# Output stores begun by ScalarE's queue instead of SyncE's, in a two-layer graph kernel

## The chip, the cores and the metric

The kernel runs on one core of a Trainium2 chip. Time is the device time of one execution in microseconds (us), smaller is better; a value is the median of several runs. The engines are TensorE (PE in the profile, with its weight loads as PEld), VectorE (DVE), ScalarE (ACT), GpSimd (POOL) and SyncE (SP). A "q" behind an engine's name means its instruction sequencer: DMA issues appear as SPq or ACTq.

## What is computed

x has 32 batches of 512 rows by 1024 columns, adj is 512 by 512, all in float32. The reference, cut to what matters:

```python
def layer0(h, wq, wk, adj, bm):            # h: (32, 512, 1024)
    q = einsum('c,bcn->bn', wq, h); k = einsum('c,bcn->bn', wk, h)
    s = leaky_relu(q[:, None, :] + k[:, :, None], 0.01)
    agg = einsum('bcn,bmn->bcm', h, softmax(s, -1))
    return relu(einsum('oc,bcm->bom', adj, agg) + bm[None, :, None])

x = x + layer0(relu(layernorm(x)), wq, wk, adj, bm)
h = relu(layernorm(x))
x = x + einsum('bnf,nm->bmf', h, adj * adj) + bias
return x
```

In layer 1 the weight W is adj squared element by element.

## The kernel before

A batch is four row tiles of 128 by 1024. The attention of layer 0 is not formed as a 1024 by 1024 matrix. Since the score is a leaky relu of a sum, the softmax splits into two sums over sorted keys. So a batch goes through these steps (the names are those of the functions and of the profile's tiles):

- `load` (L309, SP): four tiles of x. `stats`, `norm`, `slopes`, `relu` (L334 to L366): layer norm and relu.
- `scores` (L375): q and k by TensorE, copied by ScalarE (qr, L380) and stored by ScalarE's queue to DRAM (qd, L381); `row` (L386) loads them back from ScalarE's queue, broadcast over all partitions (qrow). `rank` (DVE) and `lower` (ScalarE, L433) count, for each column, its place in the sorted order.
- `value` (L474): TensorE multiplies h by adj; `spread` (L481, ScalarE) copies each result out of PSUM; `scatter` (L487, GpSimd) writes the rows in sorted order to a table in DRAM (td).
- `fetch` (L503, SP) reads the sorted table back (vs) in three pieces of 792 KB. `scan` (L559, L562) makes running sums in nine steps. In `sums` (L572 to L581) ScalarE copies a step's result out of PSUM into a tile t of a pool with two buffers. One row of it for each half is carried into the next step's operand, by ScalarE copies (L572, L573) in the first five and last four batches, and by two small SP transfers (L576, L577) in those between; two SP transfers (L580, L581) store t to the table.
- `gather` (L586, GpSimd) reads for each column three table rows (g, a pool with one buffer); `excess`, `divide`, `weigh` (L611, ScalarE), `combine` (L615, DVE) put them together; `turn` (L622, TensorE, then L626, DVE) transposes them and adds them to a second copy of x that `reload` (L314, SP) has brought (y in the profile).
- Layer 1: `stats`, `norm` and `relu` again (L337 to L366); `propagate` and `finish` (L657, L670, L674) multiply by W in a scheme with seven products, and in the last four batches `sow`, `plain` and `close` (L685, L689, L696) in the ordinary way. DVE adds each PSUM result to y in place.
- `store` (L701): when DVE has added the last piece to a row tile of y, that tile of 512 KB is written to the output. Four stores a batch, 128 in all.

The order of the work is written out by hand: ORDER is a long string of two-character codes, each of which names the next step of one lane (a step of the list above with its place in the batch). The steps of five to six batches are interleaved. The scheduler is told to keep this order (`tc.manual_schedule`), so each engine's instructions stand in its program in the order in which the steps call them, and an engine runs its program in order. A DMA is an instruction in the program of the engine that begins it, with its waits. SP begins loads, reloads, fetches, carry rows, table stores and output stores: 1442 DMAs. ScalarE begins 67, among them L381 and L386. Both engines' DMAs take eight completion semaphores in turn, in the order of the steps; a DMA waits until the earlier one with its semaphore has landed, whichever engine began that one. Tiles x, y, h and mx share a pool of 16 row buffers, so a store's landing also frees a buffer for a later load.

In a batch of the long middle part the stores stand as follows. Row 1 stands between the first and second L366 of a batch five ahead, and three loads follow it in SP's program. Row 2 stands before a copy L574, and carry rows follow it. Row 3 stands between L381 and L481. Row 0 stands between the second and third L337 of the following batch.

Of the kernel before, what the change touches and what calls it, by code (L numbers as in the profile page):

```python
# [16 lines left out]
P = 128  # L17
# [143 lines left out]
def kernel(  # L161
# [32 lines left out]
    nc = tc.nc  # L194
# [503 lines left out]
        )  # L698

    def store(s, c):  # L700
        nc.sync.dma_start(out[s.b, ts(c, P), :], s.x[c])  # L701

    lanes = {}

# [7 lines left out]
    for b in range(B):  # L712
        s = Batch()
# [37 lines left out]
        else:  # L751
            for f in (sow, plain, close):
                plan(s, f, f.__name__, args=all_of(NC, range(NH)))
        plan(s, store, "store", count=NC)
        plan(s, combine, "combine", args=all_of(NN, (1, 2)))
    names = list(lanes)
    for code in ORDER.split():
        for k in range(0, len(code), 2):
# [3 lines left out]
            s, t = args[0], len(steps)  # L762
# [31 lines left out]
```

## Time and profile before

| | us |
|---|---|
| median of 3 runs | 2302.11 (2301.16 to 2302.13) |
| profiled execution | 2301.56 |
| its span, first to last instruction | 2299.8 |
| busy: PE / ACT / DVE / POOL | 2215.1 / 1730.8 / 1719.3 / 716.9 |
| DMA | 657.77 MB, mean 286 GB/s |
| granted TensorE clock, mean | 0.988 |

| queue | begun by | share of the 16 DMA engines' time |
|---|---|---|
| q1 | SP | 46.7% |
| q0 | GpSimd (scatter, gather) | 31.3% |
| q10 | ScalarE | 2.8% |

How to read the profile's rows. A row of the timeline has the start in us from the span's beginning, the length in us, the engine, the line of the kernel, the operation, what it writes and reads with the shapes, and how many instructions are merged in it; the bracket is how long the engine stood open before and what ended that. A row of the waits has the waiting engine and line, what released it, the total in us, the number of times and the longest. A row of a stage has its bounds, its length, the busy time of PE, PEld, DVE, ACT and POOL with counts, then the granted clock, the DMA engines' mean busy share and GB/s. A row of a DMA queue has packets, MB, and the share of the 16 engines' time.

### The profile page before, as it was taken

How to read it: one execution, taken by the hardware profiler on the slowest of the kernel's cores; microseconds unless marked ns; L12 is line 12 of the kernel's file. 1: busy time of each engine (PE TensorE's matmuls, PEld its weight loads, DVE VectorE, ACT ScalarE, POOL GpSimd, SP SyncE). 2: the span in 40 equal slices, each digit the busy share in tenths (PEclk: the TensorE clock that was granted, in tenths of full speed). 3: DMA queues.
4: the chain of work that ended last, by engine and by line, in shares of the span. 5: the costliest groups of instructions: out<-in, count | busy, mean ns of one | idle time of the engine just before them, and what ended most of it. 6: DMA issues, size and time to landing. Idle time of an engine off the chain costs nothing.

```text
span 2299.8 us, 28792 instructions
## 1 busy us (share of the span) xinstructions
PE 2215.1 (96%) x7344; PEld 946.6 (41%) x7344; DVE 1719.3 (75%) x4840; ACT 1730.8 (75%) x3317; POOL 716.9 (31%) x979
## 2 busy tenths in 40 slices
PE   6978999999999999999999999999999999999897
PEld 3423443444444444444444444344444444443343
DVE  6746777878778778877877877877877787777453
ACT  4699889776778777777877777877777887787752
POOL 2343223333323333233333222333332333224210
PEclk9989999999999999999999999999999999999999
DMA  6676878888889888888888878888888888877961
GB/s 225 234 282 232 282 293 309 313 298 295 274 291 324 296 311 291 286 291 317 308 310 298 298 267 310 317 301 305 294 275 290 323 300 305 311 246 277 356 243 64
DMA packets 217717, 657.77 MB, mean 286 GB/s; under 512 B 39376, under 2 KB 39504, under 8 KB 217552
## 3 DMA queue, kind: packets, MB, share of 16 engines
q1 hardware_dynamic: 153760, 362.16, 46.7%
q0 software_dynamic: 57344, 276.86, 31.3%
q10 hardware_dynamic: 6448, 16.92, 2.8%
q8 instruction: 59, 0.97, 0.2%
q14 instruction: 106, 0.87, 0.1%
HBM read 438.05 MB, written 217.01 MB: 285 GB/s over the span
## 4 chain that ended last, share of the span: by engine, by line
PE 77%; DMA 8%; ACT 6%; DVE 5%; issue 2%; POOL 1%; SPq 0%; ACTq 0%; POOLq 0%; DVEq 0%
PE pv L474 34%; PE pg L657 26%; PE sc L562 9%; PE tr L622 3%; DMA td<-t 3%; PE pq L375 2%; DVE g L615 2%; DMA g<-td,idg 2%; PE pp L689 1%; PE sc L559 1%; ACT junk L433 1%; DVE y L626 1%; ACT junk L337 1%; DMA td<-v,idx 1%; DMA vs<-t 1%
## 5 line engine op out<-in xcount | busy, mean ns | idle before, releaser
L474 PE MATMUL pv<-wmT,x 128*128 128x512 f32 x2048 | 917.5, 596 | 0.0
L474 PEld LDWEIGHTS pv<-wmT,x 128*128 128x128 f32 x2048 | 380.5, 190 | 489.1 <-issue 452.1
L487 POOL DMA_INDIRECT td<-v,idx x256 | 270.7, 1057 | 659.5 <-issue 283.5
L657 PE MATMUL pg<-h,wsq 128*128 128x512 f32 x896 | 412.4, 602 | 2.5 <-DVE y L674 2.0
L615 DVE SCALAR_TENSOR_TENSOR g<-g,cf 128x512 f32<-128x512 f32 x512 | 375.2, 764 | 17.2 <-ACT g L611 14.0
L586 POOL DMA_INDIRECT g<-td,idg x256 | 244.8, 956 | 299.2 <-DVE y L626 95.2
L433 ACT ACTIVATE junk<-qrow,qk 128x1024 uint8<-128x1024 f32 x256 | 292.8, 1144 | 30.3 <-DMA qrow<-qd 19.9
L562 PE MATMUL sc<-vs,sm 128*64 128x512 f32 x1024 | 284.0, 621 | 7.8 <-ACT vs L572 5.8
L657 PEld LDWEIGHTS pg<-h,wsq 128*128 128x128 f32 x896 | 163.3, 190 | 243.3 <-issue 180.9
L574 ACT COPY t<-sc 128x512 f32<-128x512 f32 x288 | 167.6, 582 | 99.2 <-PE sc L562 41.6
L481 ACT COPY v<-pv 128x512 f32<-128x512 f32 x256 | 147.4, 578 | 124.3 <-PE pv L474 77.4
L546 POOL TENSOR_TENSOR sm<-mask_a,wc 128x192 f32<-128x192 f32 x96 | 63.2, 658 | 521.4 <-PE sc L562 455.9
L657 PE MATMUL pg<-mx,wmix 128*128 128x512 f32 x448 | 209.4, 599 | 0.0
L366 ACT ACTIVATE x<-x,nmr,rstd 128x1024 f32<-128x1024 f32 x128 | 149.3, 1230 | 78.2 <-DVE nmr L359 78.2
L670 DVE SCALAR_TENSOR_TENSOR y<-pg,bm_sb,y 128x512 f32<-128x512 f32 x224 | 166.4, 745 | 45.9 <-PE pg L657 45.5
L422 DVE TENSOR_SCALAR_CACHE_REDUCE junk<-qrow,qk,cnt 128x128 uint8<-128x128 f32 (+6 forms) x224 | 180.4, 805 | 8.2
L626 DVE SCALAR_TENSOR_TENSOR y<-tr,nbm,y 128x512 f32<-128x512 f32 x256 | 174.7, 746 | 15.3 <-PE tr L622 12.4
L417 DVE TENSOR_SCALAR_CACHE_REDUCE junk<-qrow,qk 128x896 uint8<-128x896 f32 (+6 forms) x224 | 165.7, 740 | 18.6 <-DMA qrow<-qd 16.7
L674 DVE TENSOR_TENSOR y<-pg,y 128x512 f32<-128x512 f32 x168 | 115.1, 685 | 81.6 <-PE pg L657 81.1
L611 ACT ACTIVATE g<-g,cf 128x512 f32<-128x512 f32 x256 | 168.6, 709 | 3.4 <-DVE cf L605 1.7
L337 ACT ACTIVATE junk<-y,nm 128x1024 uint8<-128x1024 f32 x128 | 146.7, 1146 | 31.4 <-DVE nm L345 29.6
L366 ACT ACTIVATE h<-y,nmr,rstd 128x1024 f32<-128x1024 f32 x128 | 154.0, 1235 | 2.6 <-DVE nmr L359 2.6
(135 smaller groups left out, 2496.4 us busy)
## 6 DMA issues: line engine op xcount, KB each, us to landing
vs<-td SPq DMA_DIRECT2D x96, 792.0 KB
td<-t SPq DMA_DIRECT2D x576, 132.0 KB
x<-in_x_dram SPq DMA_DIRECT2D x128, 512.0 KB
y<-in_x_dram SPq DMA_DIRECT2D x128, 512.0 KB
out_dram<-y SPq DMA_DIRECT2D x128, 512.0 KB
qrow<-qd ACTq DMA_DIRECT2D x32, 512.0 KB
vs<-t SPq DMA_DIRECT2D x368, 2.0 KB
td<-v,idx POOLq DMA_INDIRECT x256, 6.3
```

The costliest lines, as they stand in the source:

```text
L337: nc.scalar.activation(junk, s.x[c], AF.Square, bias=s.nm[:, c : c + 1], scale=1.0 / ROOT, accum_out=s.var[:, c : c + 1],)
L366: nc.scalar.activation(h, s.x[c], AF.Relu, bias=s.nmr[:, c : c + 1], scale=s.rstd[:, c : c + 1])
L422: nc.vector.tensor_scalar(junk[:, j * P :], s.qrow[:, j * P :], qc, first, ALU.is_lt, ALU.add, accum_out=s.cnt[:, 1, j : j + 1],)
L433: nc.scalar.activation(junk, s.qrow, AF.Sign, bias=s.qk[:, 1, j : j + 1], accum_out=s.sgn[:, j : j + 1])
L474: nc.tensor.matmul(pv, s.h[c][:, ts(j, P)], wmT[:, c, :], start=(c == 0), stop=(c == NC - 1))
L487: i = nc.gpsimd.indirect_dma_start(tds[s.b % TABLES][:, :], bass.IndirectOffsetOnAxis(ap=s.idx[j // 4][:, j % 4 : j % 4 + 1], axis=0), v[: ...
L562: nc.tensor.matmul(p[ts(k, HP), :], m[:, k, :], s.vs[h][:, 0:C], start=True, stop=True)
L586: nc.gpsimd.indirect_dma_start(s.g[:, j, :], None, tds[s.b % TABLES].rearrange("(s k) w -> s k w", k=3), bass.IndirectOffsetOnAxis(ap=s.id ...
L611: nc.scalar.mul(r, r, s.cf[:, 0, j : j + 1])
L615: nc.vector.scalar_tensor_tensor(r, s.g[:, j, k * W : k * W + C], s.cf[:, k, j : j + 1], r, ALU.mult, ALU.add)
L626: nc.vector.scalar_tensor_tensor(xh, pt, nbm[:, o : o + 1], xh, ALU.max, ALU.add, accum_out=s.ys[:, i, o : o + 1])
L657: nc.tensor.matmul(s.pg[key], forms[m][:, r, ts(u, P)], data, start=(m == 2 and r == 0), stop=(r == 1), skip_group_check=True,)
```

## The change

```diff
     def store(s, c):
-        nc.sync.dma_start(out[s.b, ts(c, P), :], s.x[c])
+        nc.scalar.dma_start(out[s.b, ts(c, P), :], s.x[c])
```

The 128 stores become instructions of ScalarE's program, each at the place that its step has among ScalarE's other instructions. Their transfers go through q10 and not through q1. Size, source, destination, the wait for DVE and the turn of the eight semaphores stay as they are; ORDER is unchanged.

## The prediction

> **What bounds the kernel now.** I read the page's busy shares, then the table by stages, the period of the batches from the timeline of ScalarE, the waits, and the chain.
>
> ```profile
> PE 2215.1 (96%) x7344; PEld 946.6 (41%) x7344; DVE 1719.3 (75%) x4840; ACT 1730.8 (75%) x3317; POOL 716.9 (31%) x979
> ```
>
> ```profile
> 250.00:2100.00 1850.00, 1838.15 (x6167) 785.01 (x6164) 1460.84 (x4095) 1439.45 (x2765) 597.35 (x811) 1.00 0.85 297
> 2100.00:2300.00 200.00, 168.01 (x487) 74.04 (x485) 98.94 (x216) 102.09 (x187) 33.78 (x37) 0.95 0.59 221
> ```
>
> The first number after each stage's length is TensorE's. From the first store (250 us) to 2100 us TensorE is busy 99.4%; only 12 us show as open. The last 200 us, where the last four batches drain, leave it open for 32 us, and there other work decides. Stores cover both stages, so each is costed by itself.
>
> "Busy" hides a little: the copy qr (L380), once a batch, starts at 264.64 and, 25 batches later, at 1974.15. That is 68.38 us a batch, and the shortest periods are 67.62. So the long stage holds at most 25 x 0.76 = 19 us that any cure of small waits could gain. The waits of TensorE name the place of the largest part of it in that stage:
>
> ```profile
> PE tr L622 <- ACT t L574: 5.1, 9, 0.8
> ```
>
> Nine times a transpose waits up to 0.8 us for a PSUM bank that ScalarE's copy t (L574) has not yet emptied.
>
> **The change, part by part.** 128 issues leave SP and stand in ScalarE's program at the same place of the order. Per batch four. Rows of one batch (ScalarE, then SP):
>
> ```profile
> 1008.71 4.64 ACT L366 ACTIVATE x<-x,nmr,rstd 128x1024 f32<-128x1024 f32 x4 [3.20 <-DVE nmr L359]
> 1013.71 0.59 ACT L574 COPY t<-sc 128x512 f32<-128x512 f32 x1 [0.36 <-PE sc L562]
> ...
> 1017.48 0.37 ACT L380 COPY qr<-pq 128x256 f32<-128x256 f32 x1 [2.49 <-PE pq L375]
> 1017.88 0.51 ACTq L381 DMA_DIRECT2D qd<-qr  x1
> 1021.12 0.59 ACT L481 COPY v<-pv 128x512 f32<-128x512 f32 x1 [3.27 <-PE pv L474]
> 1021.20 0.32 ACTq L386 DMA_DIRECT2D qrow<-qd  x1
> 1022.13 0.59 ACT L574 COPY t<-sc 128x512 f32<-128x512 f32 x1 [0.41 <-DMA td<-t]
> ...
> 1026.17 1.15 ACT L433 ACTIVATE junk<-qrow,qk 128x1024 uint8<-128x1024 f32 x1 [1.98 <-DMA qrow<-qd]
> ```
>
> *Issuing.* An issue on ScalarE lasts 0.32 (L386) to 0.50 us (L381): 128 x 0.32 to 0.50 = 41 to 64 us. Its cover is twofold. The issue at 1021.20 runs beside the copy of 1021.12 to 1021.71, so it need not hold the engine; and if it does, ScalarE stands open for 2299.8 - 1730.8 = 569 us. On the path: 0.
>
> *Waits, row 1 of a batch.* It stands between the first two L366 (1008.71, 1009.86); its data are ready at 1007.36. No wait.
>
> *Row 2* stands before the L574 of 1013.71. Its last DVE piece (L670) starts at 1013.22 and takes 0.74, so ScalarE is held until 1013.97 and by the issue until 1014.3 to 1014.5: L574 is 0.6 to 0.8 late. Queued behind it are three copies and then L380, which stands open 2.49 us for TensorE: the delay ends there. SP's carry rows (L576) wait for that copy and leave 0.6 to 0.8 later, but in before they lay behind three loads and this store in SP's queue until 1019.4, and the scan that reads them starts at 1020.97. On the path: 0.
>
> *Row 3* stands between L381 (1017.88) and L481 (1021.12). Its data are ready at 1017.08, but its semaphore is that of the L577 eight transfers back, which lands at 1019.59. Issued then, it ends by 1020.1, and L481 waits for TensorE until 1021.12 anyway. On the path 0 here; where SP runs about 1 us later (store of 1090.32) the semaphore comes at 1088.85 beside L481 at 1088.76, and L481 is 0.4 to 0.7 late, in front of an L574 that already waits 0.66. New is that 512 KB now lie ahead of the qrow load in ScalarE's queue. I take 0: the store starts 1.6 us earlier than before (1019.6 for 1021.30), into queues that are nearly empty there.
>
> *Row 0* stands between two L337 of 1.15 us; data and semaphore are ready when the first has just begun. 0.
>
> *What SP is freed of:* 128 issues (median 0.533 us, 2.1 us a batch). Behind row 1 stand three loads of x and behind row 2 the carry rows; they leave up to 0.55 us earlier. Bounds: no gain, if they wait for buffers and semaphores as before, and the 19 us. I take 0, since TensorE is closed in 99.4% of the stage.
>
> *The drain.* Here the end is set by gathers (POOL, L586) and what DVE and ScalarE do with them.
>
> ```profile
> 2172.45 14.68 DMA g<-td,idg
> ```
>
> ```profile
> q0 software_dynamic: 651, 3.67, 68.1%
> q1 hardware_dynamic: 684, 1.73, 33.5%
> ```
>
> The second fence is 2173 to 2186 us: gathers (q0) beside SP's queue (q1). Alone, from 2166 to 2172, q0 moved 2.12 MB in 6 us, 353 KB/us; here 282: a busy second queue costs it 71 KB/us. Before, stores stood in line with SP's other transfers and that line outlived the gather; now they are a third line. Lower bound 0 (they take from q1 alone); upper bound a second loss of 71 KB/us while 1 MB of stores goes out at q1's 1.73/13 = 133 KB/us: 7.9 us x 71 = 0.56 MB, at 282 KB/us 2.0 us. For the gather of batch 30 (stores at 2171 and 2176, with q1 busy about half that time) I take 1.0. For batch 29 (stores at 2123.8 and 2127.2 beside three fetches) nearly all, 2.0, of which 0.8 is covered, as ScalarE waits from 2146.24 to 2147.06 for a t buffer (L574): 1.2. The last gather has the same transfers finish before it in either case: 0.
>
> ScalarE's waits in the drain: batch 28 row 2 holds the copy L572 of 2152.23 until 2155.5, but the next scan starts only at 2159.20: 0. Batch 29 row 3 holds an L366 0.8 to 1.3 us at 2218.8, under the gather that lasts to 2233: 0. Batch 30 row 0 is on the chain:
>
> ```profile
> 2255.22 0.75 DVE L696 SCALAR_TENSOR_TENSOR y<-pp,bm_sb,y 128x512 f32<-128x512 f32 x1 [0.15 <-PE pp L689]
> ```
>
> Ready at 2255.97, issued by 2256.3; the L337 behind it started at 2255.73: +0.6 (bounds 0.3 to 0.8). The last four stores have nothing behind them on ScalarE.
>
> Sum: 1.2 + 1.0 + 0.6 = 2.8 on the profiled execution, 2301.56 (span 2299.8): 2304.4. The median of the runs is 0.55 above that execution, so I predict 2304.9.
>
> **Two rules against the change.** The Trainium skill, "DMA: Bandwidth & Descriptors", section "Queues, rings and completion order", has each engine go round the queues that have work, packet by packet. The drop from 353 to 282 agrees in kind; no row here has three queues busy for long. By equal turns the two gathers would pay their upper bounds and the sum would be 3.8. The Trainium skill, "Perfetto Trace Analysis", section "DMA Instruction — HWDGE (DVE, Sync)", says that a descriptor generator is locked for one DMA at a time and shared by the sequencers that issue. The trace shows 0.50 us as the usual L381 and 1.06 as its longest. By that rule the slow SP issues in the third rival would fall on ScalarE as well.
>
> **Rivals.** *Faster, SP was the brake.* For it: the period is 67.63 where SP issues row 1 at 1009.02 (1.7 us after its data) and longer, 68.36, where it does so at 1077.61 (2.6 us after); from 2100 us on SP's own waits count 101.0 us in 15 stores (L701) for DVE's L696, with table stores and reloads behind them. Against: TensorE's share. If half of the 19 us goes and the drain pays 2.8: 2302.1 - 9.5 + 2.8 = 2295.4. Decides if SP's loads leave earlier and periods reach 67.7.
>
> *Slower, row 3 goes ahead of td and qrow.* Its 512 KB now meet the td stores of 1020.09 and 1020.61 that free the t buffer for the L574 of 1023.50, and that frees a bank for TensorE's last transpose at 1026.17, 2.1 us after the copy ends. If they land over 2.1 us later, every batch pays the 0.8 of the wait above: 25 x 0.8 - 5.1 already paid = 15; in two thirds of the batches 10. With the drain 2302.1 + 10 + 2.8 = 2315. For it: td issued beside a qrow load (1089.04) landed in 4.2 us, not 2.3. Against: the store begins before them.
>
> *Slower, the slow issue moves.* The stores of 2123.76 took SP 5.66 us for two, with 2.4 MB ahead in its queue. If ScalarE pays that, its copies and L366 come 5 us later and TensorE's L689 from 2134 with them; about 3 to 5 of it is not covered: 2309.
>
> **How the numbers follow.** About 0.2% (4.6 us, 2297.5 to 2306.7) is what a measurement of this kernel can tell from no change. Forecast, the small loss: 0.46, its own range 2300 to 2306.5. SP was the brake: 0.20. Row 3 ahead: 0.22. Slow issue: 0.12. So faster 0.20, same 0.46, slower 0.34. The range takes in the first rival's 2295 and reaches 2314, short of the second's far end.
>
> **What would show it.** Right: L701 as ACTq at about 0.3 to 0.5 us; TensorE at 99% from 250 to 2100; L574 near 1013.7 of its period 0.6 to 0.8 later; gathers of batches 29 and 30 longer by 1 to 2 us. Wrong: a period that moves by over 0.2 us either way, L433 waiting over 4 us for qrow, or a chain at the end that holds ACTq L701.

## The result, and the profile after

| | before | after |
|---|---|---|
| median of the runs shown with the result, 7 each | 2302.13 (2297.51 to 2308.17) | 2310.45 (2307.72 to 2313.59) |
| ratio, 95% interval | | 1.0027 (1.0015 to 1.0040) |
| profiled execution; its span | 2301.56; 2299.8 | 2311.39; 2309.7 |

The ratio is 6.2 us (3.5 to 9.2); the two medians of seven lie 8.3 us apart. The change makes the kernel slower, by two to three times the 2.8 us that was forecast.

The page of after, its busy shares, and the table by stages (columns as in the prediction):

```profile
PE 2220.3 (96%) x7344; PEld 947.9 (41%) x7344; DVE 1718.9 (74%) x4840; ACT 1729.8 (75%) x3317; POOL 714.9 (31%) x979
```

```profile
250.00:2100.00 1850.00, 1838.78 (x6163) 784.29 (x6163) 1458.51 (x4094) 1439.34 (x2766) 595.53 (x811) 1.00 0.85 297
2100.00:2310.00 210.00, 173.94 (x491) 76.80 (x489) 101.05 (x219) 102.05 (x187) 33.72 (x37) 0.93 0.57 212
```

Between 250 and 2100 us TensorE is as busy as it was (1838.78 and 1838.15). In the drain TensorE has less clock (0.93 for 0.95). The copy qr (L380) says the same: from 264 to 1974 us it runs 1709.3 us here and 1709.5 before. So close an agreement is in part chance: in other executions with these stores on SP the stretch takes 1704.6 to 1712.3.

How late after runs against before, at points that both have, shows where the two profiled executions part:

| point | after minus before, us | added |
|---|---|---|
| copy qr of 1974 us | 0.2 | |
| last piece of the gather of batch 29 issued (2129) | 1.85 | 1.6 |
| DVE's first use of that gather (L595) | 4.45 | 2.6 |
| ScalarE's last weigh (L611) of batch 29 | 3.5 | -0.9 |
| last transpose of batch 29 (L622, 2162) | 6.7 | 3.2 |
| first use of the gather of batch 30 (2187) | 8.6 | 1.8 |
| first use of the gather of batch 31 (2233) | 8.3 | -0.3 |
| L349 behind row 0 of batch 30 (2260) | 8.9 | 0.7 |
| end | 9.9 | 0.9 |

Two single executions differ by luck too, so each of these lines was tried by itself below. A store's own issue is cheap: 339 ns in the median, 901 at most, on ScalarE (533 and 3375 on SP).

### The profile page after: what moved, and what is told of

Its sections match the earlier page's. It is cut to its first block, busy times and chain, and to the rows that moved or that the text cites. A ratio compares the mean times of both kernels' runs of the same rounds, so it can differ in the third digit from the quotient of the medians.

```text
span 2309.7 us, 28731 instructions
## 1 busy us (share of the span) xinstructions
PE 2220.3 (96%) x7344; PEld 947.9 (41%) x7344; DVE 1718.9 (74%) x4840; ACT 1729.8 (75%) x3317; POOL 714.9 (31%) x979
## 4 chain that ended last, share of the span: by engine, by line
PE 77%; DMA 8%; DVE 7%; ACT 5%; issue 2%; POOL 1%; SPq 0%; POOLq 0%; ACTq 0%; DVEq 0%
PE pv L474 35%; PE pg L657 23%; PE sc L562 9%; PE tr L622 4%; DVE g L615 3%; PE pq L375 2%; DMA g<-td,idg 2%; DMA x<-in_x_dram 2%; PE pp L689 2%; DMA vs<-t 2%; PE sc L559 1%; DMA td<-v,idx 1%; POOL g L586 1%; ACT junk L433 1%; DMA td<-t 1%
## 5 line engine op out<-in xcount | busy, mean ns | idle before, releaser
L657 PE MATMUL pg<-h,wsq 128*128 128x512 f32 x896 | 412.4, 602 | 2.9 <-DVE y L674 2.7
L586 POOL DMA_INDIRECT g<-td,idg x256 | 245.0, 957 | 269.9 <-PE tr L622 121.3
L433 ACT ACTIVATE junk<-qrow,qk 128x1024 uint8<-128x1024 f32 x256 | 292.8, 1144 | 27.6 <-DMA qrow<-qd 22.1
L562 PE MATMUL sc<-vs,sm 128*64 128x512 f32 x1024 | 285.9, 622 | 9.3 <-ACT vs L572 5.6
L657 PEld LDWEIGHTS pg<-h,wsq 128*128 128x128 f32 x896 | 163.3, 190 | 243.7 <-issue 180.4
L574 ACT COPY t<-sc 128x512 f32<-128x512 f32 x288 | 167.3, 581 | 113.9 <-PE sc L562 37.2
L546 POOL TENSOR_TENSOR sm<-mask_a,wc 128x192 f32<-128x192 f32 x96 | 62.8, 654 | 525.0 <-PE sc L562 470.6
L657 PE MATMUL pg<-mx,wmix 128*128 128x512 f32 x448 | 209.4, 599 | 0.0
L626 DVE SCALAR_TENSOR_TENSOR y<-tr,nbm,y 128x512 f32<-128x512 f32 x256 | 174.9, 747 | 20.7 <-PE tr L622 13.7
L337 ACT ACTIVATE junk<-y,nm 128x1024 uint8<-128x1024 f32 x128 | 146.8, 1147 | 31.9 <-DVE nm L345 29.4
L611 ACT ACTIVATE g<-g,cf 128x512 f32<-128x512 f32 x256 | 168.7, 710 | 2.3 <-DVE cf L605 1.8
```

The costliest lines, as they stand in the source:

```text
L433: nc.scalar.activation(junk, s.qrow, AF.Sign, bias=s.qk[:, 1, j : j + 1], accum_out=s.sgn[:, j : j + 1])
L562: nc.tensor.matmul(p[ts(k, HP), :], m[:, k, :], s.vs[h][:, 0:C], start=True, stop=True)
L574: nc.scalar.copy(t[:, 0:C], p)
L586: nc.gpsimd.indirect_dma_start(s.g[:, j, :], None, tds[s.b % TABLES].rearrange("(s k) w -> s k w", k=3), bass.IndirectOffsetOnAxis(ap=s.id ...
L611: nc.scalar.mul(r, r, s.cf[:, 0, j : j + 1])
L626: nc.vector.scalar_tensor_tensor(xh, pt, nbm[:, o : o + 1], xh, ALU.max, ALU.add, accum_out=s.ys[:, i, o : o + 1])
```

## Experiments

The theory after the result: the drain pays, by gathers that share with a third queue and by ScalarE held at a store's place; the long stage pays next to nothing. Ratios are to the kernel before on the same chip.

### The drain alone, and the rest alone

```diff
-        nc.sync.dma_start(out[s.b, ts(c, P), :], s.x[c])
+        queue = nc.scalar if s.b >= 27 else nc.sync
+        queue.dma_start(out[s.b, ts(c, P), :], s.x[c])
```

> Only the stores of batches 27 to 31 are begun by ScalarE, those of batches 0 to 26 by SyncE as before. The changed kernel took 6 us more than the kernel before (ratio 1.0027), and in its trace +0.2 of the growth had come by the qr copy (L380) of 1974 us and all the rest after. Theory, the drain pays: its stores alone give nearly all of it, +7 to +8 us on the profiled execution (the growth after 1974 us without the 1.65 that the td stores behind the stores of batch 25 cost), the gathers of batches 29 and 30 ending 2 to 3 and 1 to 2 us later after their last issue. Rival, the middle pays: the stores of 250 to 2000 us cost it by many small waits that the trace only shows as busy time, and this run lies +1 to +2 above the kernel before.

Measured: 1.0024 (1.0013 to 1.0035), 5.5 us. The other half has the two engines exchanged:

> The other half: stores of batches 0 to 26 begun by ScalarE, those of 27 to 31 by SyncE. Theory, the drain pays: 0 to +2 us against the kernel before (the stage from 264 to 1974 us again within 0.5 us of 1709.5, then at most 1.65 where the td stores of one step stand behind the two stores of batch 25), and the waits of TensorE's transposes for copy t (L574) gone again for longer waits on the carry rows. Rival, the middle pays: about +6. A third possibility, that the relief of SyncE is worth something that the drain hid: -2 to -4.

Measured: 1.0008 (0.9997 to 1.0019), 1.8 us (-0.7 to 4.4). The halves add up to 7.3 where the whole has 6.2. The drain carries most of the loss, as the theory had it, though not the 7 to 8 us that I expected; the rival that the middle carries all 6 falls, and 1.8 is small and not told from nothing.

### Waits without transfers, transfers without waits

```diff
+        if s.b >= 27:
+            peek = sp.tile([P, NH], F32, tag="peek", name=f"peek_{s.b}_{c}")
+            nc.scalar.copy(peek, s.x[c].rearrange("p (i n) -> p i n", n=HALF)[:, :, 0])
         nc.sync.dma_start(out[s.b, ts(c, P), :], s.x[c])
```

> All stores are begun by SyncE as before. For batches 27 to 31 ScalarE has, where the changed kernel has the store, a copy of 128x2 out of the finished rows into a small tile that nobody reads: it adds to the work the wait in ScalarE's order without the transfer in ScalarE's queue. Theory: the drain's growth has two parts, gathers that share with a third queue (about 4.4) and ScalarE held at a store's place (row 2 of batch 28: 2.5 to 3 with the banks that come late and the clock after it; row 0 of batch 30: 0.7 to 0.9). This run then shows the second alone: +3 to +4. Rival, only the transfers cost: 0 to +0.5. Rival, all of it is waits: +6 to +8.

Measured: 1.0000 (0.9987 to 1.0014): 0 us (-3.0 to 3.2). My 3 to 4 us for the waits fell, but for the edge of that interval; a small wait, such as the 0.7 us of row 0 of batch 30 in the table above, this run can't exclude. The timeline of ScalarE in this kernel shows the hold and its end:

```profile
2152.74 1.62 ACT L685 COPY pp<-bias_sb 128x512 f32<-128x512 f32 x3
2158.34 0.19 ACT L703 COPY peek<-y 128x2 f32<-128x2 f32 x1 [3.97 <-DVE y L696]
2158.43 0.57 ACT L572 COPY vs<-sc 1x512 f32<-1x512 f32 x1
...
2165.23 0.58 ACT L572 COPY vs<-sc 1x512 f32<-1x512 f32 x1 [4.91 <-PE sc L562]
```

L703 is the added copy. It stands 3.97 us for row 2 of batch 28 and holds the copy L572 behind it. The next L572 then stands open 4.91 us for TensorE's scan: the hold had been paid out of time that was free. Most of the 3.2 us in the table above, which I had put on it, had another cause (the last section).

```diff
+        third = (s.b, c) in ((27, 3), (27, 0), (28, 0), (28, 3))
+        queue = nc.scalar if third else nc.sync
```

> Four stores alone are begun by ScalarE: rows 3 and 0 of batch 27 and rows 0 and 3 of batch 28, those that lie beside the gathers of batches 29 and 30. None of them holds ScalarE for long. Theory: the gathers end later by 2.6 and 1.8 us, of which 0.9 of the first is covered: +3.4 to +3.5 us. Rival, the transfers only change places and what costs is ScalarE's waits: 0. By the bounds of the prediction (2.0 each, 0.8 of the first covered) +3.2.

Measured: 1.0019 (1.0007 to 1.0031), 4.4 us (1.6 to 7.1). Four of the 128 stores make most of the whole loss. The table of DMA queues from 2130 to 2137 us, under the gather of batch 29 (packets, MB, share of the 16 engines), before and then after:

```profile
q0 software_dynamic: 380, 2.12, 73.4%
q1 hardware_dynamic: 382, 0.77, 29.1%
```

```profile
q0 software_dynamic: 264, 1.47, 50.2%
q10 hardware_dynamic: 254, 0.92, 32.2%
q1 hardware_dynamic: 262, 0.55, 20.0%
```

Read the packets: two busy queues had 380 and 382, three have 264, 254 and 262. The engines take from each busy queue in equal turns, and the gather falls from one turn in two to one in three. In bytes it goes from 303 to 210 KB/us, a loss of 93, while the stores move at 131. Two stores of 0.52 MB are beside it for 8.0 us, so the gather lacks 0.74 MB, which at 303 KB/us is 2.5 us. In before the same stores stood behind SP's fetches in one line, landed at 2144.5 and 2146.3 after the gather was over, and cost it nothing; on ScalarE's queue they land at 2133.9 and 2137.8.

This is the place of the Trainium skill, "DMA: Bandwidth & Descriptors", section "Queues, rings and completion order", that the prediction weighed: each engine takes turns among the queues with work, by packets. The packet counts agree with it.

### The dose

```diff
+        queue = nc.scalar if (s.b, c) in ((27, 3), (28, 0)) else nc.sync
```

> Two stores alone are begun by ScalarE: row 3 of batch 27 and row 0 of batch 28, so one store of 512 KB beside each of the gathers of batches 29 and 30, where the run with four stores had two. From the last issue of the gather to DVE's first use (L595) the traces with these stores on SyncE had 11.6 to 11.7 us for batch 29 and 14.8 to 16.0 for batch 30, those with two stores on ScalarE 14.0 to 14.3 and 16.6 to 17.3. Theory, the gather gives way in proportion to the bytes that the third queue moves beside it: about 12.9 for batch 29 and about 16 for batch 30. Rival, a third queue that is open at all costs a fixed share: 14 and 17. Rival, the change of order behind the stores in SyncE's queue does it: 11.7 and 15.

Measured, on one execution: 12.78 us for batch 29 and 15.56 for batch 30. All executions, from the last issue of the gather (L586) to its first use (L595):

| stores beside the gather | kernels | batch 29 | batch 30 |
|---|---|---|---|
| in SP's line | nine profiled executions | 11.38 to 11.70, mean 11.55 | 14.79 to 15.99, mean 15.41 |
| one on ScalarE | this run | 12.78 | 15.56 |
| two on ScalarE | after, the drain alone, the four alone | 14.01 to 14.30, mean 14.15 | 16.63 to 17.28, mean 16.92 |

For batch 29 the loss is in proportion to the bytes: 1.2 us for one store, 2.6 for two. For batch 30 two stores cost 1.5; one costs 0.15 in this single execution, inside the spread, so there the proportion isn't shown.

### In the gather's own queue

```diff
+        if (s.b, c) in ((27, 3), (27, 0), (28, 0)):
+            held.append((s, c))          # gather(), piece 2: nc.gpsimd.dma_start for each
+            return
+        queue = nc.gpsimd if (s.b, c) == (28, 3) else nc.sync
```

> All stores by SyncE but the same four as in the run with four (rows 3 and 0 of batch 27, rows 0 and 3 of batch 28). GpSimd begins them, after the last piece of the gather of batch 29 and of batch 30: the same bytes in the gather's own queue and behind it, so that they cannot share with it. Theory: the gather of batch 29 takes 11.6 us as in the kernel before and that of batch 30 13 to 15 us (the stores no longer lie beside it in SyncE's queue); the time is -2 to 0.5 us against the kernel before. Against it: the reload of batch 30 that takes the buffer of row 0 of batch 28 starts some 9 us later and SyncE's td stores of batch 31 stand behind it; if scan copies (L574) then wait, +1 to +3. Rival, what costs is that the stores are no longer in SyncE's line, whatever queue they are in: +3 to +4, as with ScalarE.

Measured: 1.0010 (0.9996 to 1.0024), 2.3 us (-0.9 to 5.5). The stores leave just after the last piece of the gather of batch 29 (2132.75 after 2131.81). The gathers went as the theory had it; the time lies between its -2 to 0.5 and the rival's 3 to 4 and decides neither. The gathers take 11.67 and 13.33 us: not in SP's line and yet no loss for batch 29, and 2.1 us less than the mean for batch 30. So being out of SP's line isn't what costs; a further queue is. But the gain is gone again. Against before the execution is 2.8 us late at first use of batch 29, 4.5 at its last weigh and 7.1 at its last transpose: the reloads that wait for those buffers hold SP, and the td store of step 8 of batch 30 behind them leaves 1.6 us later than the lateness before it accounts for.

### The long stage: four stores back, four alone, nine back

In the long stage two traces with ScalarE's stores agreed on two places that none of the others has. The rows near 480 us of after, from the timeline of all engines:

```profile
470.70 1.22 ACTq L701 DMA_DIRECT2D out_dram<-y  x2
472.62 0.35 SPq L314 DMA_DIRECT2D y<-in_x_dram  x1
...
479.90 0.75 DVE L626 SCALAR_TENSOR_TENSOR y<-tr,nbm,y 128x512 f32<-128x512 f32 x1 [4.06 <-issue]
...
480.71 0.55 PE L622 MATMUL tr<-ident,g 128*128 128x128 f32 x3 [2.16 <-DVE y L626]
```

Two stores of batch 3 are issued ahead of the reload L314, which lands at 479.82; DVE's L626 reads it and starts at once; TensorE stands 2.16 us for that. In before the reload is ahead of both stores and lands 0.8 us before it is read.

```diff
+        keep = s.b >= 27 or (s.b, c) in ((3, 3), (3, 2), (25, 3), (25, 2))
+        queue = nc.sync if keep else nc.scalar
```

> As in the run with the stores of batches 0 to 26 from ScalarE (1.0008 of the kernel before), but four stores of them go back to SyncE: rows 3 and 2 of batch 3 and of batch 25. In both traces with ScalarE's stores in the long stage, TensorE's transposes (L622) wait 1.9 to 2.2 us near 480 us for DVE's L626, which starts as the reload of row 0 of batch 4 (L314) lands: 7.2 us after its issue with the two stores of batch 3 ahead of it, 5.3 us where they stand behind it in SyncE's order. And near 1976 to 2004 us both lose 1.1 to 1.5 us behind the two stores of batch 25. Theory, the long stage pays at these two places, where stores go ahead of a load or a td store that is soon read, and gains 1 to 2 us elsewhere: the wait on L626 near 480 is gone, batches 8 to 10 take 138 to 139.5 us by the copy qr (L380) and not 142 to 144, batches 30 to 31 lose nothing, and the time is -3 to 0 us against the kernel before. Rival, many stores cost a little each: the waits go and others come, and the time stays at about +2.

Measured: 1.0005 (0.9992 to 1.0018), 1.2 us (-1.8 to 4.1). The time doesn't tell the theory's -3 to 0 from the rival's 2. The wait for L626 is gone and batches 8 to 10 take 138.0 us. The loss near batch 31 stayed: TensorE's L657 comes about 1 us later at 2035. So rows 3 and 2 of batch 25 weren't it. The traces point to its row 0: in all four executions with that store on ScalarE it is issued beside the td stores of step 4 of batch 28, the second of them takes 8.2 to 8.5 us in place of 6.7 to 7.2, a copy L574 waits 0.9 to 1.5 us for it, and TensorE then waits 0.9 to 1.0 us ahead of an L657. No execution with the store on SP has it, but no run moves that store alone.

```diff
+        queue = nc.scalar if (s.b, c) in ((3, 3), (3, 2), (25, 3), (25, 2)) else nc.sync
```

> Four stores alone are begun by ScalarE: rows 3 and 2 of batch 3 and rows 3 and 2 of batch 25, the ones that the run before last gave back to SyncE. Theory, two places of the long stage pay: near 480 us the reload of row 0 of batch 4 lands about 7 us after its issue instead of 5.3, TensorE's L622 waits 1.9 to 2.3 us for L626, batches 8 to 10 take 141 to 144 us by the copy qr (138 to 139.5 with all stores on SyncE), and 1.1 to 1.5 us more go near 1976 to 2004 us; the time is +2 to +4 us. Rival, it needs the other stores of ScalarE too (a full queue, another spread of the completion semaphores): no such wait and 0.

Measured: 0.9999 (0.9990 to 1.0008), -0.2 us. The rival was right: the four alone cost nothing, and the reload near 480 us is issued at 471.7 and lands in 5.0 us. What delays it in after is its completion semaphore. There SP is free from 470.6 us on, but the reload follows the store of qd (L381) on its semaphore and goes 0.05 us after that lands; in before it follows a td store that had landed 0.9 us earlier. The change, then, does more than its line says: it also deals the eight semaphores out anew. Of the 1509 DMAs of SP and ScalarE 286 have another semaphore in after than in before. Each of the eight still has 188 or 189 of them, so they are dealt in turn; but with ORDER unchanged the turn differs, so it isn't set by the order of the steps alone, as the description of the kernel has it. In the kernel with the four stores beside the gathers only 4 DMAs have another one, two fetches and two of the four stores.

```diff
+        back = ((3, 3), (3, 2), (25, 3), (25, 2), (27, 3), (27, 0), (28, 0), (28, 3), (30, 0))
+        queue = nc.sync if (s.b, c) in back else nc.scalar
```

> The changed kernel with nine of its 128 stores given back to SyncE: the four of the run above, the four beside the gathers of batches 29 and 30 (rows 3 and 0 of batch 27, rows 0 and 3 of batch 28) and row 0 of batch 30. Theory, these nine carry the whole loss and the other 119 are free: the time is -2 to +1.5 us against the kernel before, the gathers of batches 29 and 30 take 11.4 to 11.7 and 14.8 to 16 us, and no transpose waits for L626 near 480. Rival, there is a loss spread over the others: +2 to +4.

Measured: 1.0004 (0.9994 to 1.0014), 0.9 us (-1.4 to 3.2); gathers 11.62 and 15.57. With nine stores back on SP the loss is no longer told from nothing; 119 stores stay on ScalarE. That the nine carry it all is not shown: by the run above the four of batches 3 and 25 cost nothing when they alone are moved, and only beside ScalarE's other stores does the wait near 480 us come with those of batch 3.

### One row of a batch alone

The sum of the long stage hides a trade. TensorE's waits between 200 and 2100 us in after, and in the kernel with batches 0 to 26 on ScalarE:

```profile
PE sc L562 <- DMA vs<-t: 2.9, 7, 0.8
...
PE tr L622 <- DVE y L626: 2.2, 1, 2.2
PE tr L622 <- ACT t L574: 0.4, 1, 0.4
```

```profile
PE sc L562 <- DMA vs<-t: 6.6, 11, 1.6
...
PE tr L622 <- DVE y L626: 1.9, 1, 1.9
```

The wait that the prediction led with, L622 for the copy t (L574), 5.1 us before and 3.8 to 7.9 in the executions with these stores on SP (6.1 in the expectation below leaves out the run with the gather's own queue), is gone. In its place scans (L562) wait 2.9 and 6.6 us for the carry rows vs, where before had 1.0. I put the gain on row 3 and the loss on row 2:

```diff
+        queue = nc.scalar if c == 3 and 6 <= s.b <= 24 else nc.sync
```

> Only the stores of row 3 of batches 6 to 24 are begun by ScalarE (19 of 128). In the traces with all stores on SyncE TensorE's transposes L622 wait 3.8 to 6.1 us in all for ScalarE's copy t (L574) between 200 and 2100 us, and the scans (L562) 0.8 to 3.1 us for the carry rows; in those with the stores of batches 6 to 24 on ScalarE it is 0 to 1.0 and 1.2 to 6.6. Theory, two effects of two rows that cancel: row 3 stood in SyncE's queue ahead of the td stores of two scan steps, the second of which (L581) leaves 5.9 us after the copy qr instead of 8.4 and so frees the t buffer that L574 waits for; row 2 holds ScalarE 0.8 us ahead of an L574 whose carry rows a scan soon reads. With row 3 alone the wait for L574 falls to 0 to 1.5 us, the scans' wait stays at 0.8 to 3, and the time is -5 to -1.5 us against the kernel before. Rival, the spread of the eight completion semaphores, not the place in the queue, sets when that td store leaves: it waits as before and the time is the same within 1.5.

```diff
+        queue = nc.scalar if c == 2 and 6 <= s.b <= 24 else nc.sync
```

> Only the stores of row 2 of batches 6 to 24 are begun by ScalarE. Theory, as for the run with row 3: row 2 alone pays. The L574 before each copy qr comes 0.7 to 0.8 us later, the carry rows of the second of its two copies (L576, L577) land about 1 us later, the scans' wait for them grows from about 1 to 3 to 7 us, the transposes' wait for L574 stays at 4 to 6, and the time is +1 to +5 us. Rival, the prediction's own step for this row: the delay ends at the copy qr and costs nothing, 0.

Measured: 1.0105 (1.0083 to 1.0128), 24 us, for row 3, and 1.0093 (1.0067 to 1.0118), 21 us, for row 2. Nineteen stores of the 128 cost three to four times what all of them cost. For row 3 both my theory and its rival were wrong, the theory in the sign too; for row 2 the sign was right, and the largest size that I gave four times too small. The first has the transposes' wait down, as expected, and the carry rows' up. TensorE's waits for row 3 and then row 2:

```profile
PE sc L562 <- DMA vs<-t: 18.1, 23, 2.0
...
PE tr L622 <- ACT t L574: 0.2, 1, 0.2
```

```profile
PE sc L562 <- DMA vs<-t: 11.4, 9, 2.8
PE tr L622 <- ACT t L574: 4.8, 10, 1.1
```

SP's own waits from 690 to 1850 us tell why; before, after, row 3, row 2:

```profile
SPq L581 <- DMA qrow<-qd: 40.4, 16, 3.1
...
SPq L576 <- DMA x<-in_x_dram: 14.0, 16, 1.5
```

```profile
SPq L576 <- DMA x<-in_x_dram: 13.2, 14, 1.9
```

```profile
SPq L576 <- DMA out_dram<-y: 12.2, 15, 1.1
```

```profile
SPq L576 <- DMA out_dram<-y: 33.0, 15, 3.6
```

None of these pairs shares data. L581 stores t to the table and has nothing to do with qrow; L576 moves a row of t and has nothing to do with a load of x or a store of y. What they share is a semaphore. Every DMA issue in the trace names its own, so the previous user can be looked up; medians over 18 batches, in us from the start of that batch's copy qr:

| | before | after | row 3 alone | row 2 alone |
|---|---|---|---|---|
| td store L581 of step 8: issued | 8.45 | 5.86 | 6.65 | 6.46 |
| its semaphore is that of | qrow load | a td store | a td store | a td store |
| it lands | 10.96 | 9.28 | 9.43 | 10.72 |
| first carry row L576 of step 0: issued | 0.71 | 1.04 | 2.13 | 2.45 |
| its semaphore is that of | a load of x | a load of x | store of row 2 | store of row 2 |
| it lands | 3.27 | 4.37 | 4.89 | 4.06 |
| second carry row L577 of step 0: lands | 3.70 | 4.53 | 5.09 | 4.74 |
| transposes wait for L574 / scans (L562) for carry rows | 5.1 / 1.0 | 0.4 / 2.9 | 0.2 / 18.1 | 4.8 / 11.4 |

In 15 of the 18 batches before's L581 goes within 0.12 us of the landing of qrow; in after it never waits for it. That alone isn't the gain of 4.7 us: with row 2 alone L581 leaves early too, but lands at 10.72, and the transposes wait 4.8 us as before. The wait is gone in the two kernels in which the store of row 3 no longer lies ahead of L581 in SP's line; there L581 lands at 9.28 and 9.43.

The loss is in the carry rows. The scan of step 1 needs both, and where nothing delays it it starts 4.40 us after the copy qr. In before they land in time; in after the second lands at 4.53, and the scans wait a little. In 15 of 18 batches of both single-row kernels L576 goes within 0.12 us of the landing of store row 2, and everything behind it in SP's program, the second carry row included, goes later. With row 3 alone the scan then waits 0.2 to 0.9 us at nearly every batch. But most of the time goes in a few batches. One of them, with row 3 alone (L702 is the store there):

```profile
1509.87 0.53 SPq L576 DMA_DIRECT2D vs<-t  x1
1510.56 0.53 SPq L577 DMA_DIRECT2D vs<-t  x1
1510.62 0.34 ACTq L386 DMA_DIRECT2D qrow<-qd  x1
...
1512.02 1.04 PE L562 MATMUL sc<-vs,sm 128*64 128x512 f32 x2 [0.72 <-DMA vs<-t]
...
1514.83 1.83 PE L562 MATMUL sc<-vs,sm 128*64 128x512 f32 x2 [1.77 <-DMA vs<-t]
```

Here L577 leaves beside the qrow load of 512 KB, and its 2 KB land 4.2 us later, 0.17 us after that load. In both single-row kernels every second carry row of step 0 that was issued no earlier than 0.22 us before the qrow load took 3.5 to 4.7 us and landed 0.16 to 0.34 us after that load, six with row 3 and five with row 2; the others were issued at least 0.3 us before it and took 1.6 to 3.0. In after none is that late. The six batches are 19 us longer than in before, of 23 for the stage from 264 to 1974 us, and the five 14 of 19; in five of these eleven half clock follows the wait. So a store's landing that holds a carry row by 1 to 2 us costs little, unless it pushes the row back to the qrow load. By which rule the semaphores are dealt, no run here shows.

### The kernel before again

> The kernel before once more, unchanged, for a second profile. In the first one TensorE had its full clock from 2155 to 2160 us and ran the matmuls of L689 there in 3.60 us, where every other trace so far has the clock at 0.5 for a part of it and loses 1.1 to 2.6 us. If the half clock is a matter of the execution and not of the stores, this profile may show it there too; gather 29 takes 11.6 to 11.7 us, gather 30 14.8 to 16, and the stretch of batches 8 to 10 138 to 139.5.

Measured, on one execution: 2303.28; gathers 11.43 and 15.54, batches 8 to 10 in 138.5 us, and the full clock at its L689 near 2157 us. So the half clock didn't show here. Over all fourteen executions five kept the clock there (both of before, both with one row alone, the one with nine back: 2.6 to 2.7 us from the end of the last combine to that of the last transpose) and nine lost it for a part (3.7 to 5.1 us), among them four with all the drain's stores on SP. So the loss comes without these stores too; but all four executions with a store on ScalarE beside the gather of batch 29 have it.

## Why the prediction was right or wrong, step by step

The time lies in the range, and the forecast step, gathers that share with a third queue, is the main cause. The sign "slower", at 0.34, was the second likeliest; the forecast itself, 2304.9 with its own range to 2306.5, was too low.

- **Issuing, 0: right.** 339 ns a store, and stores beside copies. The rival "the slow issue moves" is out: the two stores after 2123 us took SP 5.6 us together, ScalarE 0.41 and 0.50.
- **Gather of batch 29, +2.0 with 0.8 covered: mis-sized.** It is +2.6 with 0.9 covered, 1.65. The term that failed is the rate, and with it the upper bound: I took the loss to a third queue to be at most that to a second, 71 KB/us; it is 93, and the 3.8 that the prediction gave for equal turns still used the 71. Its principle, that what stood in line is now beside the gather, is what the experiments show.
- **Gather of batch 30, +1.0: mis-sized**, 1.5. Gather of batch 31, 0: right (15.6 against 15.4 to 16.1 in executions with the drain's stores on SP).
- **Row 2 of batch 28 holds L572, 0: right**, and after the result I doubted it wrongly; the copy came 3.6 us late for nothing that the run with waits alone could tell.
- **Row 0 of batch 30, +0.6: right.** The store goes at 2264.28 and the L337 behind it at 2264.67; the lateness grows by 0.67 in after and in the drain alone, by nothing in nine other executions with that store on SP and no copy in its place, and by 0.27 in a tenth.
- **Long stage, row 2 delays L574 by 0.6 to 0.8 and costs 0: the size right, the "0" wrong.** L574 comes 0.80 us later (median; mean 0.69). The prediction looked at the carry rows of the first of the two copies, which a scan reads at 1020.97. Those of the second, needed 4.40 us after the copy qr, it left out; they land 1.1 and 0.8 us later, and scans wait for them 2.9 us in place of 1.0. The delay doesn't end at L380.
- **What SP is freed of, and row 3, 0: wrong.** The td store L581 of step 8 lands 1.7 us earlier without row 3 ahead of it in SP's line, and the wait of 5.1 us went to 0.4. This and the carry rows nearly cancel, so that the stage's sum, 0, is near the 1.8 (-0.7 to 4.4) that was measured. That was luck more than insight.
- **The turn of the semaphores**, which the change's description has stay as it is. The prediction used the semaphore of one store (that of the L577 eight transfers back) and took all others as unchanged. They are dealt anew: in after that delays the reload near 480 us, and the runs with one row alone show that it can be worth 20 us, more than any step of the sum. It isn't behind after's late carry rows: L576 follows a load of x there as in before, and is issued 0.3 us later.
- **Row 0 of batch 25** was costed at 0 with all rows 0. By the traces it shares with td stores and costs about 1 us.
- **Rivals.** "SP was the brake" has a true core (4.7 us of waits) and the wrong sum. "Row 3 goes ahead of td and qrow" is out: the td store of step 8 lands at 9.28 us and not 10.96, and L433 waits for qrow 22.1 us in all, against 19.9.
- **Signs of being wrong.** Two that the prediction named came, once each: L433 waits 4.19 us for qrow at 480 us, and the chain at the end holds an ACTq L701, 0.34 us at 2267.71. The first lies in the place of the late reload; the second is a store issued just ahead of the L349 behind row 0 of batch 30.

The ledger, then, of the 6.2 us: gathers 1.65 and 1.5, row 0 of batch 30 0.7, long stage 1.8, together 5.6. The rest is within the interval. The half clock has a part in it that these runs don't settle: from the last combine to the last transpose of batch 29 it takes 4.4 us in the mean of the three executions with two stores beside the gather, and 3.4 in the nine without. By that difference an estimate of its part is 1.0, which would also bring the run with the four stores alone, 4.4, near its two gathers, 3.15.

None of these kernels is shown to be faster than before. The one that I expected to be, row 3 alone, is the slowest.

## What to carry to other kernels

A transfer moved to an idle queue doesn't become free: where it stood in line behind others it now takes equal turns with whatever is in flight, so look for what the end waits on in that stretch (here a gather), and count its turns with one more queue. Before counting on a DMA's wait as unchanged, look up whose completion semaphore it follows in both traces: moving one issue can hand a short transfer the semaphore of a long one, and what that delays may then fall beside a larger load. And a stage whose busy share doesn't move may hold two equal and opposite waits, which the waits by releaser show and the sum hides.

## What the hardware showed that I had not expected

TensorE's clock. Stages of after and of before, one step of 3.41 us a row (busy TensorE is the first number after the length, the granted clock the third from the end):

```profile
2154.06:2157.47 3.41, 0.66 (x2) 0.28 (x2) 3.41 (x7) 0.56 (x2) 0.00 (x0) 1.00 1.02 408
2157.47:2160.88 3.41, 2.65 (x11) 2.53 (x12) 3.17 (x9) 1.51 (x3) 0.00 (x0) 0.50 0.41 165
```

```profile
2150.11:2153.53 3.42, 2.65 (x16) 0.72 (x14) 3.42 (x6) 2.26 (x5) 0.00 (x0) 1.00 1.03 414
2153.53:2156.94 3.41, 2.48 (x14) 1.77 (x15) 3.41 (x9) 0.68 (x2) 0.00 (x0) 1.00 0.95 372
```

TensorE stands open here three times in after, for 2.06, 0.99 and 1.00 us, and twice in before, for 0.70 and 0.99. In before the steps of 3.41 us hold 2.65 and 2.48 us of work each, and the clock stays. In after one holds 0.66, and from the next row on the clock is 0.50 for 6.8 us: eight matmuls L689 take 5.53 us for 3.60, and the step from the last combine to the last transpose 2.5 us longer, most of the 3.2 us that I had first put on the held copy. Over the fourteen profiled executions, from 150 us on, every step with full clock and at most 1.42 us of TensorE's work was followed by half clock, every one with 1.54 or more kept it, and the few between went either way; at half clock, every step with 2.86 us or more was followed by the full clock and none with 2.82 or less. At this place the five executions that kept the clock stand open 1.3 to 1.9 us in all ahead of these transposes, the nine that lost it 2.4 to 4.1, and the loss costs 1.1 to 2.5 us. What the nine have more is one stand, for DVE's L696: 1.2 to 2.1 us in the four with a store on ScalarE beside the gather, 2.1 in the run with the gather's own queue, and 0.4 to 0.6 in the four with all the drain's stores on SP. The Trainium skill, "TensorE: Matmul & The Clock Gate", section "Part 1: The HAM clock gate (the "warmup" mystery)", has a free-running window of this length and half clock after an idle one; the rows agree with the window, and show that it needn't be idle: steps with up to 1.42 us of work in 3.41 were followed by half clock too.
